# Graph attention on one core: row sums by a transposing VectorE sum and a 32-column product, score runs of four key tiles on three PSUM buffers, fixed issue order

## The chip, the core and the metric

The kernel runs on one core of a Trainium2 chip. The metric is the device time of one execution in microseconds (us). Three runs of the kernel before took 3753.75, 3755.6 and 3756.18 us.

The engines are named as in the profile: PE multiplies matrices (PEld is its weight load), DVE is the vector engine, ACT the scalar engine, POOL the general-purpose engine, SP the engine whose queue issues all DMAs here. Each engine works through its own instructions in order and waits on semaphores for the others. PE writes to PSUM, from which DVE and ACT read; POOL reads and writes SBUF.

## What is computed

A layer norm with ReLU, then attention with eight heads of 64 over a graph's adjacency, and a residual add. `x` is 16 x 1024 x 512, `adj` 1024 x 1024, the weights 512 x 512, all float32.

```python
def reference(x, adj, Wq, bq, Wk, bk, Wv, bv):
    h = jnp.maximum(_layernorm(x), 0.0)
    q, k, v = ((h @ W + b).reshape(16, 1024, 8, 64) for W, b in ((Wq, bq), (Wk, bk), (Wv, bv)))
    scores = jnp.einsum('bihd,bjhd->bhij', q, k) / jnp.sqrt(jnp.float32(64))
    scores = scores + jnp.where(adj == 0, -1e9, 0.0)[None, None, :, :]
    weights = jax.nn.softmax(scores, axis=-1)
    return x + jnp.einsum('bhij,bjhd->bihd', weights, v).reshape(16, 1024, 512)
```

## The kernel before

`main_path` does everything; after it, `all_rows_fine` checks the row sums, and `general_path` stands ready for data whose sums are out of bounds, which these are not.

An iteration `i` (there are 128: 16 images, 4 pairs of heads, 2 halves of the queries) works on one image `b`, one pair of heads `p` and 512 queries `qh`. For each of the eight key tiles `kt`, `scores` (L159 to L173) makes a score tile of 128 keys by 2 heads by 512 queries: PE makes two products of 64 rows each (L164), one for each head, which lie on different halves of PE's rows; DVE adds the mask on the way out of PSUM (L167); ACT takes the exponential in place (L168); POOL adds the tile into an accumulator `a` of 128 by 1024 (L171, L173). The scores lie transposed, keys on the partitions, so the sum over the keys is a sum over tiles and then over partitions.

One iteration later, `weighted_sum` (L175) multiplies the eight tiles by V into one PSUM tile `po` (L182: 32 instructions, two abreast in different column halves) and multiplies the accumulator by a matrix of ones (L193, `pr`), so that every one of 64 rows of the result holds the sum over the partitions. ACT copies both out (L195, L197). `finish` (L205) turns the sums (L209, `prt`) and the output (L218, `pot`) into rows of queries by PE transposes; DVE takes the sums (L212), their reciprocals (L214) and the scaled output (L220), POOL adds the residual `xr` (L225), SP stores it.

Between the scores stand fillers that prepare what comes next: three projections an iteration in most (L133 `pk`, L140 `pq`, L149 `pv`, eight instructions of 512 columns each), the transposes of the next image's normed `x` (L125 `pht`, out by ACT, L126), and its loads and norm (`load_norm`: load, statistics on DVE, power on POOL, shift on DVE, ReLU on ACT). `fillers(i)` deals them over the four quarters of an iteration, each behind two score tiles. This is the order in which the program is written; a scheduler then orders each engine's instructions, and may move one between the two products of a score tile.

PSUM has eight banks: two score tiles of two banks each (`ps_s`), one bank for `po` and one for `pr` (`ps_o`), and two for everything else (`ps_a`, tag `acc`): the projections and all transposes take these two in turn. A tile's owner has to wait until the engine that reads the last one but one has done so.

Of the kernel before, what the change touches and what calls it, by code (L numbers as in the profile page):

```python
# [36 lines left out]
def main_path(tc, x, adj, Wq, bq, Wk, bk, Wv, bv, out, sums):  # L37
# [9 lines left out]
    with ExitStack() as ctx:  # L47
        pool = lambda name, bufs=1, **k: ctx.enter_context(tc.tile_pool(name=name, bufs=bufs, **k))
        const = pool("const")
        xpool = pool("xpool", 4)  # L50
# [12 lines left out]
        X, HT, Q, K, V = {}, {}, {}, {}, {}  # L63
# [10 lines left out]
        ones = const.tile([P, HD], F32, tag="ones", name="ones")  # L74
        nc.gpsimd.memset(ones, 1.0)
# [30 lines left out]
        def norm(b, t):  # L106
# [3 lines left out]
            shift = small.tile([P, 1], F32, tag="shift", name=f"shift_{b}_{t}")  # L110
            nc.vector.bn_stats(st, X[b, t])  # L111
            nc.vector.bn_aggr(mv, st)
            nc.vector.tensor_scalar_add(rstd, mv[:, 1:2], EPS)
            nc.gpsimd.tensor_tensor(rstd, rstd, minus_half, ALU.pow)
            nc.vector.scalar_tensor_tensor(shift, mv[:, 0:1], -1.0, rstd, op0=ALU.mult, op1=ALU.mult)  # L115
            nc.scalar.activation(X[b, t], X[b, t], AF.Relu, bias=shift, scale=rstd)  # L116
# [36 lines left out]
        PR, ACC, OT, RS, XR = {}, {}, {}, {}, {}  # L153
# [21 lines left out]
        def weighted_sum(i):  # L175
            b, p, qh = where(i)
            po = ps_o.tile([P, 512], F32, tag="o", name=f"po_{i}")
# [11 lines left out]
            pr_sum = ps_o.tile([P, 512], F32, tag="r", name=f"pr_{i}")  # L189
            acc = ACC.pop(i)  # L190
            for r in range(2):
                rows = slice(r * HD, r * HD + HD)
                nc.tensor.matmul(pr_sum[rows, :], ones, acc[:, r, :], start=True, stop=True)  # L193
# [10 lines left out]

        def finish(i):  # L205
            pt = ps_a.tile([P, TH, P], F32, tag="acc", name=f"prt_{i}")
            rs = RS.pop(i)
            for t in range(TH):
                nc.tensor.transpose(pt[:, t, :], rs[:, ts(t, P)], ident)  # L209
            s = sums[:, i, :]  # L210

            nc.vector.tensor_scalar(s.rearrange("q (t r) -> q t r", r=2), pt[:, :, 0:P:HD], 2.0**-60, None, op0=ALU.max)  # L212
            inv = small.tile([P, 2 * TH], F32, tag="inv", name=f"inv_{i}")
            nc.vector.reciprocal(inv, s)  # L214
            pt = ps_a.tile([P, TH, P], F32, tag="acc", name=f"pot_{i}")
            ot = OT.pop(i)
            for t in range(TH):
                nc.tensor.transpose(pt[:, t, :], ot[:, ts(t, P)], ident)  # L218
            o = work.tile([P, TH, P], F32, tag="o", name=f"o_{i}")
            nc.vector.tensor_mul(  # L220
                o.rearrange("q t (r d) -> q (t r) d", r=2),
                pt.rearrange("q t (r d) -> q (t r) d", r=2),
                inv[:, :, None].to_broadcast([P, 2 * TH, HD]),
            )
            nc.gpsimd.tensor_tensor(o, o, XR.pop(i), ALU.add)  # L225
            nc.sync.dma_start(rows_of(out, i), o)


        def fillers(i):

# [13 lines left out]
            out = [[], [], [], []]  # L244
            for place, g in zip((0, 2, 3), groups):
                out[place].append(g)
            if i:
                out[1].append((weighted_sum, i - 1))
                out[2].append((finish, i - 1))
            flips = {0: (0, 1), 1: (2,), 2: (3,), 3: (4,), 4: (5,), 5: (6, 7)}  # L250
            if b + 1 < B:
                for n, t in enumerate(flips.get(j, ())):
                    out[0 if n == 0 else 3].insert(0, (flip, b + 1, t))

                for t in ((2, 3), (4,), (5,), (6,), (7,), ())[j] if j < 6 else ():
                    out[1].append((load_norm, b + 1, t))
            if j == 6 and b + 2 < B:
                out[1] += [(load_norm, b + 2, 0)]
            if j == 7 and b + 2 < B:
                out[1] += [(load_norm, b + 2, 1)]  # L260
            return out

        def load_norm(b, t):
            load_x(b, t)
            norm(b, t)


        for t in range(NT):
            if t >= 2:
                load_x(0, t)  # L270
            norm(0, t)
# [10 lines left out]
        if B > 1:  # L282
            load_norm(1, 0)
            load_norm(1, 1)
# [9 lines left out]
        weighted_sum(total - 1)  # L294
        finish(total - 1)

# [180 lines left out]
```

## Time and profile before

| | |
|---|---|
| median of three runs | 3755.6 us |
| the profiled execution's own time | 3754.31 us |
| its span, first to last instruction | 3752.5 us |
| granted PE clock | 0.998 |
| PE busy | 3711.6 us, 99% |
| POOL busy | 2337.1 us, 62% |
| DVE busy | 1657.9 us, 44% |
| ACT busy | 1482.8 us, 40% |
| first weighted sum starts at | 109.8 us |

The profile comes from one execution. A row of a group gives line, engine, operation, output and inputs, shape and count, then the busy time in us, the mean ns of one instruction, and the engine's idle time ahead of them with what ended it. A row of a timeline gives start, length, engine, line, operation and count, and in brackets the idle time before it. PE's lengths include the drain of its pipe, so neighbours overlap; the time that a piece takes of PE is the next piece's start less its own.

### The profile page before, as it was taken

How to read it: one execution, taken by the hardware profiler on the slowest of the kernel's cores; microseconds unless marked ns; L12 is line 12 of the kernel's file. 1: busy time of each engine (PE TensorE's matmuls, PEld its weight loads, DVE VectorE, ACT ScalarE, POOL GpSimd, SP SyncE). 2: the span in 40 equal slices, each digit the busy share in tenths (PEclk: the TensorE clock that was granted, in tenths of full speed). 3: DMA queues.
4: the chain of work that ended last, by engine and by line, in shares of the span. 5: the costliest groups of instructions: out<-in, count | busy, mean ns of one | idle time of the engine just before them, and what ended most of it. 6: DMA issues, size and time to landing. Idle time of an engine off the chain costs nothing.

```text
span 3752.5 us, 34865 instructions
## 1 busy us (share of the span) xinstructions
PE 3711.6 (99%) x13378; PEld 1437.4 (38%) x13378; DVE 1657.9 (44%) x2190; ACT 1482.8 (40%) x1681; POOL 2337.1 (62%) x1161
## 2 busy tenths in 40 slices
PE   7999999999999999999999999999999999999998
PEld 3333333333333333333333333333333333333333
DVE  3444444444444444444444444444444444443444
ACT  3433434343343334334333343343433434333343
POOL 1666666666666666666666666666666666666676
PEclk9999999999999999999999999999999999999999
DMA  3001001000100010001000110010101001100000
GB/s 124 26 28 29 26 27 33 23 29 27 32 26 23 29 34 26 26 23 35 27 26 26 30 30 26 26 31 26 29 26 31 29 23 29 31 29 17 17 23 24
DMA packets 157709, 110.58 MB, mean 29 GB/s; under 512 B 7392, under 2 KB 138464, under 8 KB 157536
## 3 DMA queue, kind: packets, MB, share of 16 engines
q1 hardware_dynamic: 157536, 108.30, 9.8%
q8 instruction: 106, 1.74, 0.2%
q14 instruction: 67, 0.55, 0.0%
HBM read 74.72 MB, written 33.55 MB: 29 GB/s over the span
## 4 chain that ended last, share of the span: by engine, by line
PE 98%; DVE 1%; issue 0%; DMA 0%; POOL 0%; SPq 0%; ACT 0%; DVEq 0%; POOLq 0%; ACTq 0%
PE ps L164 29%; PE po L182 24%; PE pk L133 12%; PE pv L149 12%; PE pq L140 12%; PE pr L193 3%; PE pot L218 2%; PE pht L125 2%; PE prt L209 1%; DVE p L167 0%; DMA x<-in_x_dram 0%; PE pmask L102 0%; POOL a L173 0%; SPq L90 0%; SPq L83 0%
## 5 line engine op out<-in xcount | busy, mean ns | idle before, releaser
L173 POOL TENSOR_TENSOR a<-a,p 128x1024 f32<-128x1024 f32 x768 | 1808.4, 2355 | 1017.7 <-ACT p L168 987.0
L167 DVE TENSOR_TENSOR p<-ps,mask 128x1024 f32<-128x1024 f32 x1024 | 1206.2, 1219 | 1093.6 <-PE ps L164 1093.1
L168 ACT ACTIVATE p<-p 128x1024 f32<-128x1024 f32 x1024 | 1082.3, 1057 | 1210.7 <-DVE p L167 1182.2
L164 PE MATMUL ps<-qT,kT 64*128 64x512 f32 x4096 | 1157.9, 619 | 4.8 <-DVE p L167 4.8
L182 PE MATMUL po<-p,v 128*64 128x512 f32 x4096 | 907.2, 595 | 0.0
L164 PEld LDWEIGHTS ps<-qT,kT 64*128 64x128 f32 x4096 | 386.6, 185 | 590.1 <-issue 504.0
L171 POOL TENSOR_TENSOR a<-p,p 128x1024 f32<-128x1024 f32 x128 | 300.9, 2350 | 353.1 <-ACT p L168 353.1
L182 PEld LDWEIGHTS po<-p,v 128*64 128x64 f32 x4096 | 282.8, 137 | 608.7 <-issue 595.0
L133 PE MATMUL pk<-hT,wk 128*128 128x512 f32 x1024 | 471.9, 604 | 0.2 <-ACT mask L103 0.2
L149 PE MATMUL pv<-wv,hT 128*128 128x512 f32 x1024 | 470.2, 603 | 0.0
L140 PE MATMUL pq<-hT,wq 128*128 128x512 f32 x1024 | 464.4, 596 | 0.0
L133 PEld LDWEIGHTS pk<-hT,wk 128*128 128x128 f32 x1024 | 184.1, 189 | 268.7 <-issue 267.5
L149 PEld LDWEIGHTS pv<-wv,hT 128*128 128x128 f32 x1024 | 184.6, 190 | 266.6 <-issue 266.6
L140 PEld LDWEIGHTS pq<-hT,wq 128*128 128x128 f32 x1024 | 184.5, 190 | 212.2 <-issue 212.2
L116 ACT ACTIVATE x<-x,shift,rstd 128x512 f32<-128x512 f32 x128 | 103.8, 813 | 386.2 <-DVE shift L115 382.8
L195 ACT COPY ot<-po 128x512 f32<-128x512 f32 x128 | 74.9, 585 | 455.3 <-PE po L182 455.3
L150 DVE TENSOR_TENSOR v<-pv,bv_rows 128x512 f32<-128x512 f32 x128 | 88.4, 690 | 242.6 <-PE pv L149 242.6
L111 DVE BATCH_NORM_STATS2 st<-x 128x6 f32<-128x512 f32 x128 | 88.5, 691 | 221.2 <-DMA x<-in_x_dram 221.2
L225 POOL TENSOR_TENSOR o<-o,xr 128x512 f32<-128x512 f32 x128 | 162.4, 1269 | 2.5 <-DVE o L220 0.7
L220 DVE TENSOR_TENSOR o<-pot,inv 128x512 f32<-128x512 f32 x128 | 88.5, 692 | 142.2 <-PE pot L218 141.7
L134 ACT ACTIVATE kT<-pk,bk_cols 128x512 f32<-128x512 f32 x128 | 87.9, 687 | 126.6 <-PE pk L133 126.6
L193 PE MATMUL pr<-a,ones 128*64 128x512 f32 x512 | 131.7, 593 | 2.6 <-POOL a L173 2.6
(38 smaller groups left out, 920.1 us busy)
## 6 DMA issues: line engine op xcount, KB each, us to landing
x<-in_x_dram SPq DMA_DIRECT2D x128, 256.0 KB, 2.6
xr<-in_x_dram SPq DMA_DIRECT2D x128, 256.0 KB, 3.0
out_dram<-o SPq DMA_DIRECT2D x128, 256.0 KB, 2.2
adj<-in_adj_dram SPq DMA_DIRECT2D x8, 512.0 KB, 7.1
wk<-in_L_gnn_Wk_dram SPq DMA_DIRECT2D x1, 1024.0 KB, 7.3
wq<-in_L_gnn_Wq_dram SPq DMA_DIRECT2D x1, 1024.0 KB, 9.3
wv<-in_L_gnn_Wv_dram SPq DMA_DIRECT2D x1, 1024.0 KB, 11.5
bv_rows<-in_L_gnn_bv_dram SPq DMA_DIRECT2D x1, 256.0 KB, 10.0
```

Of the source, the lines that this page charges most:

```text
L116: nc.scalar.activation(X[b, t], X[b, t], AF.Relu, bias=shift, scale=rstd)
L133: nc.tensor.matmul(acc, W["k"][:, c, ts(p, P)], HT[b, hf][:, c, :], start=(c == 0), stop=(c == DC - 1))
L140: nc.tensor.matmul(acc, W["q"][:, c, ts(p, P)], HT[b, hf][:, c, :], start=(c == 0), stop=(c == DC - 1))
L149: nc.tensor.matmul(acc, HT[b, hf][:, c, ts(tt, P)], W["v"][:, c, :], start=(c == 0), stop=(c == DC - 1))
L164: nc.tensor.matmul(ps[:, r, :], K[b, p][rows, ts(kt, P)], Q[b, p, qh][rows, :], start=True, stop=True)
L167: nc.vector.tensor_tensor(pr, ps, m[:, None, :].to_broadcast([P, 2, 512]), ALU.add)
L168: nc.scalar.activation(pr, pr, AF.Exp, scale=HD**-0.5)
L171: nc.gpsimd.tensor_tensor(ACC[i], PR[i, 0], pr, ALU.add)
L173: nc.gpsimd.tensor_tensor(ACC[i], ACC[i], pr, ALU.add)
L182: nc.tensor.matmul(po[rows, :], V[b][:, kt, p * P + r * HD : p * P + r * HD + HD], pr[:, r, :], start=(kt == 0), stop=(kt == NT - 1),)
L193: nc.tensor.matmul(pr_sum[rows, :], ones, acc[:, r, :], start=True, stop=True)
L225: nc.gpsimd.tensor_tensor(o, o, XR.pop(i), ALU.add)
```

## The change

- **Row sums.** `pr` and its 64-column products with ones are gone, as are its copy by ACT and the four PE transposes `prt`. Instead DVE sums the accumulator with `apply_transpose`: each block of 32 by 32 is transposed and summed along what had been the partitions, which leaves 128 x 32 partial sums `rs`, one for each quarter of the partitions. A new step `row_sums` adds the quarters by one product of 32 columns with a 128 x 128 matrix `same` (one where two indices agree modulo 32); DVE picks each query's own quarter out of it (`picked`), sums, and takes the reciprocal.
- **PSUM.** Three score tiles instead of two. `ps_o` is gone; `po` takes its turn in `ps_a`.
- **Order.** An iteration has two halves of four score tiles each. Behind the first come the x transpose, one projection, the weighted sum of the iteration before, its DVE sum, a second x transpose if there is one, the statistics, and loads; behind the second the row sums, the norm, two projections and the output. PE, DVE, ACT and POOL keep this order as written (`manual_schedule`); SP is still scheduled.
- **Loads** of `x` are issued an iteration ahead of their statistics, from five buffers instead of four; the norm is split into `stats` and `norm`.

```diff
-        xpool = pool("xpool", 4)
+        xpool = pool("xpool", 5)
...
-        ps_s = pool("ps_s", 2, space=psum)
-        ps_o = pool("ps_o", 1, space=psum)
+        ps_s = pool("ps_s", 3, space=psum)
...
+        nc.vector.tensor_reduce(place, ident.rearrange("p (g q) -> p q g", q=32), AX.X, ALU.add)
+        nc.vector.tensor_reduce(group, ident.rearrange("p (g q) -> p g q", q=32), AX.X, ALU.add)
+        nc.vector.tensor_copy(same.rearrange("p (g q) -> p g q", q=32), place[:, None, :].to_broadcast([P, 4, 32]))
+        nc.vector.tensor_copy(own, group[:, None, :].to_broadcast([P, 2 * TH, 4]))
...
         def weighted_sum(i):
             b, p, qh = where(i)
-            po = ps_o.tile([P, 512], F32, tag="o", name=f"po_{i}")
+            po = ps_a.tile([P, 512], F32, tag="acc", name=f"po_{i}")
...
-            pr_sum = ps_o.tile([P, 512], F32, tag="r", name=f"pr_{i}")
-            acc = ACC.pop(i)
-            for r in range(2):
-                rows = slice(r * HD, r * HD + HD)
-                nc.tensor.matmul(pr_sum[rows, :], ones, acc[:, r, :], start=True, stop=True)
+            RS[i] = small.tile([P, 4 * 2 * TH], F32, tag="rs", name=f"rs_{i}")
+            acc = ACC.pop(i).rearrange("p r (c q) -> p (r c) q", q=32)
+            nc.vector.tensor_reduce(RS[i], acc, AX.X, ALU.add, apply_transpose=True)
             OT[i] = work.tile([P, 512], F32, tag="ot", name=f"ot_{i}")
             nc.scalar.copy(OT[i], po)
-            RS[i] = work.tile([P, 512], F32, tag="rs", name=f"rs_{i}")
-            nc.scalar.copy(RS[i], pr_sum)
...
+        def row_sums(i):
+            pt = ps_a.tile([P, 2 * TH, 4], F32, tag="acc", name=f"pr_{i}")
+            nc.tensor.matmul(pt.rearrange("q a g -> q (a g)"), same, RS.pop(i), start=True, stop=True)
+            s = sums[:, i, :]
+            picked = small.tile([P, 2 * TH, 4], F32, tag="picked", name=f"picked_{i}")
+            nc.vector.scalar_tensor_tensor(picked, pt, 2.0**-60, own, op0=ALU.max, op1=ALU.mult)
+            nc.vector.tensor_reduce(s, picked, AX.X, ALU.add)
+            INV[i] = small.tile([P, 2 * TH], F32, tag="inv", name=f"inv_{i}")
+            nc.vector.reciprocal(INV[i], s)
...
         def finish(i):
-            pt = ps_a.tile([P, TH, P], F32, tag="acc", name=f"prt_{i}")
-            rs = RS.pop(i)
-            for t in range(TH):
-                nc.tensor.transpose(pt[:, t, :], rs[:, ts(t, P)], ident)
...
+        LOADS = ((4,), (5,), (6,), (7,), (), (0,), (1,), (2, 3))
+        STATS = ((2, 3), (4,), (5,), (6,), (7,), (), (0,), (1,))
+        FLIPS = ((0, 1), (2,), (3,), (4,), (5,), (6, 7), (), ())
...
+            first = flips[:1] + groups[:1]
             if i:
+                first.append((weighted_sum, i - 1))
+            first += flips[1:] + [(stats, *bt) for bt in normed] + loads
+            second = [(row_sums, i - 1)] if i else []
+            second += [(norm, *bt) for bt in normed] + groups[1:]
+            if i:
+                second.append((finish, i - 1))
+            return first, second
...
-        for i in range(total):
-            fill = fillers(i)
-            for quarter in range(4):
-                scores(i, 2 * quarter)
-                scores(i, 2 * quarter + 1)
-                for f, *a in fill[quarter]:
-                    f(*a)
+        with tc.manual_schedule(engines={engines.PE, engines.DVE, engines.Activation, engines.Pool}):
+            for i in range(total):
+                fill = fillers(i)
+                for half in range(2):
+                    for kt in range(half * NT // 2, (half + 1) * NT // 2):
+                        scores(i, kt)
+                    for f, *a in fill[half]:
+                        f(*a)
```

PE before, in the third iteration of the first image, from the product with ones to the second `pk` (a row is one line of the program, `x2` its products; numbers at the ends of names are the program's own):

```order
L193 MATMUL pr_784<-a_601,ones 64x512 x2
L164 MATMUL ps_4_805<-qT_1_0_609,kT_1_556 128x512 x2
L164 MATMUL ps_5_812<-qT_1_0_609,kT_1_556 128x512 x2
L133 MATMUL pk_2_0_820<-hT_0_131,wk 128x512 x4
L209 MATMUL prt_826<-ident,rs_789 128x128 x4
L164 MATMUL ps_6_843<-qT_1_0_609,kT_1_556 128x512
L218 MATMUL pot_834<-ident,ot_787 128x128 x4
L164 MATMUL ps_6_843<-qT_1_0_609,kT_1_556 128x512
L164 MATMUL ps_7_850<-qT_1_0_609,kT_1_556 128x512 x2
L133 MATMUL pk_2_1_857<-hT_1_202,wk 128x512 x4
```

PE now, in the same iteration, from the last rows of the weighted sum to the next iteration's first score tile:

```order
L192 MATMUL po_770<-p_7_693,v_406 64x512 x2
L174 MATMUL ps_4_802<-qT_1_0_630,kT_1_583 128x512 x2
L174 MATMUL ps_5_809<-qT_1_0_630,kT_1_583 128x512 x2
L174 MATMUL ps_6_816<-qT_1_0_630,kT_1_583 128x512 x2
L174 MATMUL ps_7_823<-qT_1_0_630,kT_1_583 128x512 x2
L215 MATMUL pr_830<-rs_787,same 128x32
L143 MATMUL pk_2_0_841<-hT_0_134,wk 128x512 x4
L143 MATMUL pk_2_1_847<-hT_1_205,wk 128x512 x4
L229 MATMUL pot_853<-ident,ot_789 128x128 x4
L174 MATMUL ps_0_862<-qT_1_1_763,kT_1_583 128x512 x2
```

Four score tiles stand together and whole, where there were two, then one cut in two by `pot`, then one; `prt` is gone, and `pr` is one product of 32 columns behind the run.

DVE before, in the same iteration, from the statistics of `x` to the output's scaling (`p` is a mask add, `qT` a projection's way out of PSUM):

```order
L111 BN_STATS st_7_1069<-x_7_1067 128x6
L112 BN_AGGR mv_7_1070<-st_7_1069 128x2
L113 TENSOR_SCALAR rstd_7_1071<-mv_7_1070 128x1
L141 TENSOR_SCALAR qT_1_1_746<-pq_1_1_747,bq_cols 128x512
L115 SCALAR_TENSOR_TENSOR shift_7_1072<-mv_7_1070,rstd_7_1071 128x1
L167 TENSOR_TENSOR p_2_756<-ps_2_753,mask 128x1024
L167 TENSOR_TENSOR p_3_763<-ps_3_760,mask 128x1024
L167 TENSOR_TENSOR p_4_808<-ps_4_805,mask 128x1024
L167 TENSOR_TENSOR p_5_815<-ps_5_812,mask 128x1024
L212 TENSOR_SCALAR sums<-prt_826 128x8
L214 RECIPROCAL inv_832<-sums 128x8
L220 TENSOR_TENSOR o_839<-pot_834,inv_832 128x512
```

DVE now, from the last add of the first half to the work on the row sums:

```order
L177 TENSOR_TENSOR p_3_753<-ps_3_750,mask 128x1024
L151 TENSOR_SCALAR qT_1_1_763<-pq_1_1_764,bq_cols 128x512
L202 TENSOR_REDUCE rs_787<-a_608 128x32
L116 BN_STATS st_5_793<-x_5_667 128x6
L117 BN_AGGR mv_5_794<-st_5_793 128x2
L118 TENSOR_SCALAR rstd_5_795<-mv_5_794 128x1
L177 TENSOR_TENSOR p_4_805<-ps_4_802,mask 128x1024
L177 TENSOR_TENSOR p_5_812<-ps_5_809,mask 128x1024
L177 TENSOR_TENSOR p_6_819<-ps_6_816,mask 128x1024
L177 TENSOR_TENSOR p_7_826<-ps_7_823,mask 128x1024
L219 SCALAR_TENSOR_TENSOR picked_832<-pr_830,own 128x32
L220 TENSOR_REDUCE sums<-picked_832 128x8
```

The new sum of the accumulator stands between the way out of `qT` and the second half's adds, and the work on the sums behind the last add; the shift has moved behind them too.

More of the change, by code (lines that the diff above doesn't have):

```diff
@@ L114, in norm @@
             nc.gpsimd.tensor_tensor(rstd, rstd, minus_half, ALU.pow)
+            MV[b, t], RSTD[b, t] = mv, rstd
+        def norm(b, t):
+            mv, rstd = MV.pop((b, t)), RSTD.pop((b, t))
+            shift = small.tile([P, 1], F32, tag="shift", name=f"shift_{b}_{t}")
             nc.vector.scalar_tensor_tensor(shift, mv[:, 0:1], -1.0, rstd, op0=ALU.mult, op1=ALU.mult)
@@ L220, in finish @@
             nc.vector.tensor_mul(
[L221 to L223 removed]
+                o.rearrange("q t (r d) -> q t r d", r=2),
+                pt.rearrange("q t (r d) -> q t r d", r=2),
+                inv.rearrange("q (r t) -> q t r", r=2)[:, :, :, None].to_broadcast([P, TH, 2, HD]),
             )
```

56 lines of the change are left out of this document (23 added, 33 removed).

## The prediction

> **What bounds the kernel now.** I read the page first: the engines' busy times and the chain of work that ended last.
>
> ```profile
> span 3752.5 us, 34865 instructions
> PE 3711.6 (99%) x13378; PEld 1437.4 (38%) x13378; DVE 1657.9 (44%) x2190; ACT 1482.8 (40%) x1681; POOL 2337.1 (62%) x1161
> PE 98%; DVE 1%; issue 0%; DMA 0%; POOL 0%; SPq 0%; ACT 0%; DVEq 0%; POOLq 0%; ACTq 0%
> PE ps L164 29%; PE po L182 24%; PE pk L133 12%; PE pv L149 12%; PE pq L140 12%; PE pr L193 3%; PE pot L218 2%; PE pht L125 2%; PE prt L209 1%; DVE p L167 0%; DMA x<-in_x_dram 0%; PE pmask L102 0%; POOL a L173 0%; SPq L90 0%; SPq L83 0%
> ```
>
> PE is the chain. Busy can hide waiting, so I asked for the stretch from the first weighted sum to the start of the last, by the windows view:
>
> ```profile
> core 0: us, PE busy (x) PEld busy (x) DVE busy (x) ACT busy (x) POOL busy (x), PEclk, DMA share, GB/s
> 109.83:3729.34 3619.51, 3615.43 (x13059) 1391.85 (x13057) 1612.90 (x2093) 1439.96 (x1622) 2301.39 (x1126) 1.00 0.09 27
> ```
>
> These are 127 iterations of 3619.51/127 = 28.50 us (28.9 in the full ones, below), at full clock, with 4 us of PE idle in all. So only PE's own order and amount of work can pay, and only as long as no other engine makes PE wait. The timeline of PE over one full iteration shows what the 28.90 us go to (start, length, what; pieces overlap by their drain, so I use differences of starts):
>
> ```profile
> 695.70 1.99 PE L164 MATMUL ps<-qT,kT 64*128 64x512 f32 x8
> 697.61 3.70 PE L149 MATMUL pv<-wv,hT 128*128 128x512 f32 x8
> 701.15 0.60 PE L209 MATMUL prt<-ident,rs 128*128 128x128 f32 x4
> 701.68 1.12 PE L164 MATMUL ps<-qT,kT 64*128 64x512 f32 x2
> 702.74 0.66 PE L218 MATMUL pot<-ident,ot 128*128 128x128 f32 x4
> 703.32 1.98 PE L164 MATMUL ps<-qT,kT 64*128 64x512 f32 x6
> 705.23 0.66 PE L125 MATMUL pht<-ident,x 128*128 128x128 f32 x4
> 705.73 3.60 PE L149 MATMUL pv<-wv,hT 128*128 128x512 f32 x8
> 709.25 1.99 PE L164 MATMUL ps<-qT,kT 64*128 64x512 f32 x8
> 711.17 3.70 PE L140 MATMUL pq<-hT,wq 128*128 128x512 f32 x8
> 714.80 1.99 PE L164 MATMUL ps<-qT,kT 64*128 64x512 f32 x8
> 716.72 7.09 PE L182 MATMUL po<-p,v 128*64 128x512 f32 x32
> 723.64 1.03 PE L193 MATMUL pr<-a,ones 128*64 128x512 f32 x4
> 724.60 0.70 PE L164 MATMUL ps<-qT,kT 64*128 64x512 f32 x2
> ```
>
> The beat of a 512-column step is in the weight loads of the weighted sum, which come two abreast (one pair of 64-column products a step):
>
> ```profile
> 688.73 0.14 PEld L182 LDWEIGHTS po<-p,v 128*64 128x64 f32 x2 [0.29 <-issue]
> 689.16 0.14 PEld L182 LDWEIGHTS po<-p,v 128*64 128x64 f32 x2 [0.29 <-issue]
> ```
>
> So a step is 0.43 us. A score tile is four instructions in two steps, its two 64-row products side by side. Three things stand out. A run of two tiles (x8) takes 1.92, four steps (1.72) and 0.20: the price of entering and leaving the 64-row mode, about 0.10 at each end (pr before scores shows one end: 0.96 against two steps, 0.86). The tile that the output transposes (pot) cut in two takes 1.06 for its lone half, two steps and the mode's price; the x6 behind pot takes as long as x8. And pr and prt are PE work for row sums alone.
>
> **The change, part by part.**
>
> PE's scores. Today an iteration has five runs: 1.91 + 1.06 + 1.91 + 1.92 + 1.92 = 8.72. In the new fixed order there are two runs of four whole tiles: 2 x (8 x 0.43 + 0.20) = 7.28. Saved 1.44.
>
> Row sums on PE. pr goes: 0.96, of which 0.10 is the mode's price that the weighted sum now pays on its way to the scores: saved 0.86. prt goes: 0.53 + 0.58 for prt and pot now, against 0.44 + 0.09 for pot alone with one exit: saved 0.58. The projections no longer each border a run: 3.54 + 3.52 + 3.63 = 10.69 against 3.43 + 3.43 + 3.53: saved 0.30. New is the product of 32 columns with the 128x128 weights "same": two instructions. No row shows such a form. The nearest are a transpose of 128 columns, four steps in 0.44 (pht above: 705.23 to 705.73, with 0.06 for the mode), so 0.11 each, and the closing count's product of 2 columns:
>
> ```profile
> L419 PE MATMUL c_n<-c_both,c_ones 128*1 128x2 f32 x2 | 0.2, 164 | 3.3 <-issue 3.3
> ```
>
> Both of its instructions end within 0.2 us. I take two steps of 0.11 and 0.03 for the waiting weights, 0.25, and 0.10 for entering full mode in the projections' place: 0.35; ends 0.1 and 0.6. [...]
>
> Together 1.44 + 0.86 + 0.58 + 0.30 - 0.35 = 2.83 us an iteration. Two iterations in eight have a second x transpose between weighted sum and scores, 0.2 each, 0.05 on the mean.
>
> Does a wait take it back? Durations and latencies that decide this:
>
> ```profile
> L173 POOL TENSOR_TENSOR a<-a,p 128x1024 f32<-128x1024 f32 x768 | 1808.4, 2355 | 1017.7 <-ACT p L168 987.0
> L168 ACT ACTIVATE p<-p 128x1024 f32<-128x1024 f32 x1024 | 1082.3, 1057 | 1210.7 <-DVE p L167 1182.2
> L225 POOL TENSOR_TENSOR o<-o,xr 128x512 f32<-128x512 f32 x128 | 162.4, 1269 | 2.5 <-DVE o L220 0.7
> L114 POOL TENSOR_TENSOR rstd<-rstd,minus_half 128x1 f32<-128x1 f32 x128 | 70.0, 548 | 30.1 <-DVE rstd L113 29.9 <-DVE shift L115 0.2
> L126 ACT COPY hT<-pht 128x512 f32<-128x512 f32 x128 | 72.7, 568 | 30.5 <-PE pht L125 30.5
> L111 DVE BATCH_NORM_STATS2 st<-x 128x6 f32<-128x512 f32 x128 | 88.5, 691 | 221.2 <-DMA x<-in_x_dram 221.2
> L167 DVE TENSOR_TENSOR p<-ps,mask 128x1024 f32<-128x1024 f32 x1024 | 1206.2, 1219 | 1093.6 <-PE ps L164 1093.1
> L411 DVE TENSOR_REDUCE c_both<-sums 128x1 f32<-128x1024 f32 x1 | 1.2, 1209 | 0.0
> L214 DVE RECIPROCAL inv<-sums 128x8 f32<-128x8 f32 x128 | 26.0, 203 | 4.4
> L212 DVE TENSOR_SCALAR sums<-prt 128x8 f32<-128x8 f32 x128 | 20.5, 160 | 164.5 <-PE prt L209 164.5
> ```
>
> And from the DVE timeline, how soon it follows PE (scores from 695.70, pot from 702.74, pq from 711.17), with a place near the end where runs stand close and two buffers run out, and the whole of such waits from the waits view (total, times, longest):
>
> ```profile
> 696.94 2.36 DVE L167 TENSOR_TENSOR p<-ps,mask 128x1024 f32<-128x1024 f32 x2 [6.59 <-PE ps L164]
> 703.43 0.69 DVE L220 TENSOR_TENSOR o<-pot,inv 128x512 f32<-128x512 f32 x1 [1.07 <-PE pot L218]
> 714.91 0.75 DVE L141 TENSOR_SCALAR qT<-pq,bq_cols 128x512 f32<-128x512 f32 x1
> 3589.13 2.34 DVE L167 TENSOR_TENSOR p<-ps,mask 128x1024 f32<-128x1024 f32 x2
> 3590.39 0.30 PEld L164 LDWEIGHTS ps<-qT,kT 64*128 64x128 f32 x4 [1.78 <-DVE p L167]
> 3590.39 2.26 PE L164 MATMUL ps<-qT,kT 64*128 64x512 f32 x8 [0.95 <-DVE p L167]
> PE ps L164 <- DVE p L167: 4.8, 6, 1.0
> ```
>
> *Fourth tile of a run.* Let a run start at 0. The first mask add starts at 1.24 (695.70 to 696.94) and ends at 2.46; two adds in 2.36 mean one each 1.14. PE reaches tile four at 0.10 + 6 x 0.43 = 2.68. Released PE loads weights 0.04 after the add's end (3589.13 + 1.22, then 3590.39), so at 2.50, and needs 0.10 more: 2.60. With three buffers the wait is nothing, by a margin of 0.08 alone. In the first run of an iteration pot's multiply stands ahead on DVE: it starts 0.69 after pot, ends at 1.38, and the run's first add is due at 0.53 + 1.24 = 1.77 on that clock. Covered by 0.4. If the margin fails, a run pays at most 0.27 (2.26 against 1.99 above).
>
> *The weighted sum's PSUM.* It now shares two buffers with the projections and takes the one that the x transpose left, which ACT copies out behind all four exponentials: adds end at 1.24 + 3 x 1.14 + 1.22 = 5.88, the last exponential at 6.97, the copy at 7.55. PE is there at 3.64 + 0.50 + 3.53 = 7.67. Margin 0.12; nothing counted, up to 0.2 in the upper bound. ACT is relieved of the rs copy.
>
> *DVE's sum.* Behind qT on DVE (starts at 4.14 + 3.74 = 7.88, ends 8.6) stand the transposing sum of 1024 columns and the statistics (0.69 and two small ones of the size of the sums' rows, 1.0), before the second run's first add at 7.67 + 7.0 + 1.24 = 15.9. The sum may last 15.9 - 8.6 - 1.0 = 6.3 us before it delays anything. The row of the plain 1024-column reduce says 1.2, which I take; a transposing one is in no row, so the upper end is open (a rival, below). It waits for POOL's last add: POOL needs 7 x 2.35 + 0.55 + 1.27 = 18.3 of 26.1 us, starts the second run's four adds at 14.7 + 3.6 = 18.3 and ends them at 27.8, 1.7 into the next iteration; DVE asks at 8.6. Hidden. The three small operations on the sums come behind the last add of the second run: the first, which frees the PSUM buffer, ends at about 6.1 from that run's start, and the second projection, which takes the buffer, is due at 3.64 + 0.35 + 3.43 = 7.4.
>
> *Loads.* They are issued one iteration ahead of their statistics, with five buffers, and SP has them ahead of the output stores that wait for POOL; DVE's waits for x (221 us in the st row) were hidden and go. Worth nothing; if SP held one back, DVE would stand before the second run's adds with the slack of 6.3 - 1.2 = 5.1 us.
>
> I put the small margins at 0.03 a run. An iteration then saves 2.83 - 0.05 - 0.06 = 2.72. In the last eight intervals there are few projections or none; eight score tiles then follow each other and DVE's 1.14 a tile rules against 0.86, so I count half there: 119 x 2.72 + 8 x 1.36 = 335. Prologue and tail: nothing. The profiled execution took 3754.3 (span 3752.5), so 3754.3 - 335 = 3419; the median of the runs is 1.3 above that execution, which makes **3420 us**, 9% less.
>
> Bounds: all waits nil and the small product at its 0.1 gives 0.25 + 0.06 more, 39 us, 3381; both runs paying 0.27, the weighted sum 0.2 and the product 0.6 takes 0.54 + 0.2 + 0.25 = 1.0 us, 126, up to 3546 if all come together.
>
> **Rivals.**
>
> *New waits inside the runs.* DVE lags by a few tenths in every run (through pot's multiply, v's evacuation or a slower release), and PE stands at the fourth tile or at the weighted sum. For it: margins of 0.08 and 0.12, in-order queues. Against: only six such waits before, 4.8 us. At 0.4 a run, 0.8 an iteration: 3420 + 102 = 3522.
>
> *DVE becomes the bound: slower.* If the transposing sum works its 32 blocks one at a time, its price is 32 times a small instruction. From 6.3 us each further us costs 127; from 6.3 + 2.7 = 9.0 the kernel is slower than now. At 32 x 0.33 = 10.6 us: 3420 + 4.3 x 127 = 3966. For it: no row has the form. Against: the plain reduce is 1.2, and DVE's smallest rows (0.16 to 0.2) would give 6.4 even block by block. [...]
>
> *No change.* The gain is eaten exactly: a sum of about 9 us, or waits of 2.7 an iteration. 3754. That the change might not do what it says is excluded by the two orders, which show whole tiles and no pr or prt.
>
> **How the numbers follow.** Forecast (3380 to 3460) 0.72; waits in the runs (3460 to 3600) 0.20; slower 0.05; no change 0.03. The range 3380 to 3495 takes in the forecast and the nearer half of the first rival, 0.82. Faster by over 0.2% (7.5 us, what a measurement of this kernel can tell from none): 0.92; within: 0.03; slower: 0.05.
>
> **What would show it.** Right: the weighted sums start 26.1 us apart in full iterations; a run x16 of scores takes 3.64; the small product under 0.4; the transposing sum about 1.2; PE's waits for DVE stay under 20 us in all. Wrong: score rows on PE with idle time released by DVE's mask add; a sum above 6 us; PE waiting on POOL for row sums.

## The result, and the profile after

The changed kernel takes 3402.35 us (median of four runs, 3402.22 to 3403.19), the kernel before 3754.68 us beside it: a ratio of 0.906, interval 0.9046 to 0.9078. It is 9.4% faster; the forecast was 3420, 9% less. The profiled execution's span is 3400.4 us against 3752.5, 352.1 less.

From the page of the profile after, its busy times, its chain and four groups (line, engine, operation, shape and count; busy us, mean ns of one; idle us ahead of them and what ended it):

```profile
PE 3359.0 (99%) x12610; PEld 1365.5 (40%) x12610; DVE 1998.0 (59%) x2450; ACT 1414.9 (42%) x1553; POOL 2338.3 (69%) x1160
PE 97%; DVE 1%; POOL 1%; issue 1%; SPq 0%; DMA 0%; ACT 0%; DVEq 0%; POOLq 0%; ACTq 0%
L174 PE MATMUL ps<-qT,kT 64*128 64x512 f32 x4096 | 953.2, 603 | 5.3 <-DVE p L177 5.2
L183 POOL TENSOR_TENSOR a<-a,p 128x1024 f32<-128x1024 f32 x768 | 1811.3, 2359 | 782.8 <-ACT p L178 732.6
L202 DVE TRANSPOSE_TENSOR_REDUCE rs<-a 128x32 f32<-128x1024 f32 x128 | 158.0, 1234 | 9.8 <-POOL a L183 9.8
L125 DVE SCALAR_TENSOR_TENSOR shift<-mv,rstd 128x1 f32<-128x1 f32 x128 | 226.3, 1777 | 2.6 <-POOL rstd L119 2.6
```

PE still is the chain, and its busy time fell by 352.6 us, which is the whole difference of the spans. So nothing was gained from waits and next to nothing lost to them: over all 4096 score instructions PE stood 5.2 us for DVE's mask add. The transposing sum takes 1.234 us. One row is odd: `shift`, an operation on one column, takes 1777 ns where it took 159; it comes up again below.

PE's timeline over one full iteration after (start, length, what), from the small product of one iteration to that of the next:

```profile
640.36 0.41 PE L215 MATMUL pr<-rs,same 128*128 128x32 f32 x2
640.60 7.11 PE L159 MATMUL pv<-wv,hT 128*128 128x512 f32 x16
647.55 0.60 PE L229 MATMUL pot<-ident,ot 128*128 128x128 f32 x4
648.08 3.70 PE L174 MATMUL ps<-qT,kT 64*128 64x512 f32 x16
651.72 3.70 PE L150 MATMUL pq<-hT,wq 128*128 128x512 f32 x8
655.35 7.09 PE L192 MATMUL po<-p,v 128*64 128x512 f32 x32
662.37 3.70 PE L174 MATMUL ps<-qT,kT 64*128 64x512 f32 x16
666.00 0.41 PE L215 MATMUL pr<-rs,same 128*128 128x32 f32 x2
```

Read by differences of starts: a run of four tiles (x16) takes 3.64 and 3.63, the small product 0.24, pot 0.53, and from product to product it is 25.64 us (an iteration without an x transpose). DVE's timeline in the second half of the same stretch:

```profile
655.46 0.75 DVE L151 TENSOR_SCALAR qT<-pq,bq_cols 128x512 f32<-128x512 f32 x1 [1.51 <-PE pq L150]
656.12 1.24 DVE L202 TRANSPOSE_TENSOR_REDUCE rs<-a 128x32 f32<-128x1024 f32 x1
657.28 0.65 DVE L116 BATCH_NORM_STATS2 st<-x 128x6 f32<-128x512 f32 x1
...
663.61 4.62 DVE L177 TENSOR_TENSOR p<-ps,mask 128x1024 f32<-128x1024 f32 x4 [5.27 <-PE ps L174]
668.70 2.24 DVE L125 SCALAR_TENSOR_TENSOR shift<-mv,rstd 128x1 f32<-128x1 f32 x1
```

The sum follows qT without a wait, and behind the statistics DVE stands idle for 5.27 us until the next run's first tile: the slack in which a longer sum would disappear. The windows view splits the stretch between the first and the last weighted sum at the 120th, for the kernel before and for the one after (us, PE busy, clock, DMA share, GB/s):

```profile
109.83:3548.13 3438.30, 3438.30 (x12370) 1.00 0.09 27
3548.13:3729.34 181.21, 177.13 (x691) 1.00 0.07 21
```

```profile
107.36:3211.38 3104.02, 3103.87 (x11656) 1.00 0.10 30
3211.38:3378.08 166.70, 160.81 (x642) 1.00 0.08 23
```

Over 119 intervals the mean goes from 28.89 to 26.08 us: 334.3 us saved. The last eight save 14.5, the prologue 2.5 (the first weighted sum starts at 107.36 instead of 109.83), the tail 0.8.

### The profile page after: what moved, and what is told of

It is laid out like the page before. It is cut to its first block, busy times and chain, and to the rows that moved or that the text cites. A ratio compares the mean times of both kernels' runs of the same rounds, so it can differ in the third digit from the quotient of the medians.

```text
span 3400.4 us, 33496 instructions
## 1 busy us (share of the span) xinstructions
PE 3359.0 (99%) x12610; PEld 1365.5 (40%) x12610; DVE 1998.0 (59%) x2450; ACT 1414.9 (42%) x1553; POOL 2338.3 (69%) x1160
## 4 chain that ended last, share of the span: by engine, by line
PE 97%; DVE 1%; POOL 1%; issue 1%; SPq 0%; DMA 0%; ACT 0%; DVEq 0%; POOLq 0%; ACTq 0%
PE ps L174 27%; PE po L192 26%; PE pq L150 13%; PE pk L143 13%; PE pv L159 13%; PE pht L135 2%; PE pot L229 2%; PE pr L215 1%; POOL a L183 1%; DVE p L177 0%; PE pmask L108 0%; DMA x<-in_x_dram 0%; SPq L89 0%; DVE st L116 0%; SPq L96 0%
## 5 line engine op out<-in xcount | busy, mean ns | idle before, releaser
L177 DVE TENSOR_TENSOR p<-ps,mask 128x1024 f32<-128x1024 f32 x1024 | 1182.2, 1217 | 750.7 <-PE ps L174 750.7
L174 PE MATMUL ps<-qT,kT 64*128 64x512 f32 x4096 | 953.2, 603 | 5.3 <-DVE p L177 5.2
L174 PEld LDWEIGHTS ps<-qT,kT 64*128 64x128 f32 x4096 | 365.1, 186 | 486.7 <-issue 346.2
L143 PE MATMUL pk<-hT,wk 128*128 128x512 f32 x1024 | 455.3, 597 | 0.0
L159 PE MATMUL pv<-wv,hT 128*128 128x512 f32 x1024 | 454.4, 597 | 0.0
L151 DVE TENSOR_SCALAR qT<-pq,bq_cols 128x512 f32<-128x512 f32 x128 | 96.1, 751 | 235.0 <-PE pq L150 235.0
L125 DVE SCALAR_TENSOR_TENSOR shift<-mv,rstd 128x1 f32<-128x1 f32 x128 | 226.3, 1777 | 2.6 <-POOL rstd L119 2.6
L202 DVE TRANSPOSE_TENSOR_REDUCE rs<-a 128x32 f32<-128x1024 f32 x128 | 158.0, 1234 | 9.8 <-POOL a L183 9.8
```

The costliest lines, as they stand in the source:

```text
L143: nc.tensor.matmul(acc, W["k"][:, c, ts(p, P)], HT[b, hf][:, c, :], start=(c == 0), stop=(c == DC - 1))
L159: nc.tensor.matmul(acc, HT[b, hf][:, c, ts(tt, P)], W["v"][:, c, :], start=(c == 0), stop=(c == DC - 1))
L174: nc.tensor.matmul(ps[:, r, :], K[b, p][rows, ts(kt, P)], Q[b, p, qh][rows, :], start=True, stop=True)
L177: nc.vector.tensor_tensor(pr, ps, m[:, None, :].to_broadcast([P, 2, 512]), ALU.add)
L202: nc.vector.tensor_reduce(RS[i], acc, AX.X, ALU.add, apply_transpose=True)
```

## The experiments

Each was timed beside the kernel before, whose medians lay between 3753.3 and 3753.8. The theory: PE's order and amount of work pay, term by term as in the prediction, and the fixed order and the third buffer only keep the other engines out of its way. The rivals: the row sums alone bring most of it; DVE's sum or its place is close to becoming the bound; the order is worth nothing.

| label | kernel | us | ratio to before, interval |
|---|---|---|---|
| row_sums_only | before, with the new row sums | 3696.34 | 0.985 (0.9819 to 0.9876) |
| runs_only | after, with the old row sums | 3528.30 | 0.940 (0.9373 to 0.9427) |
| runs_of_two | after, score runs of two tiles | 3471.53 | 0.925 (0.9222 to 0.9276) |
| runs_of_two_two_buffers | the same on two score buffers | 3474.94 | 0.926 (0.9231 to 0.9284) |
| two_score_buffers | after, on two score buffers | 3672.41 | 0.978 (0.9755 to 0.9812) |
| product_x3 | after, small product three times | 3457.66 | 0.921 (0.9192 to 0.9229) |
| sum_x5 | after, DVE's sum five times | 3407.87 | 0.908 (0.906 to 0.9096) |
| sum_x8 | after, DVE's sum eight times | 4075.26 | 1.086 (1.0834 to 1.0877) |
| shift_one_tensor | after, another form of `shift` | 3400.98 | 0.906 (0.9045 to 0.9075) |
| sum_early | after, DVE's sum half an iteration earlier | 4355.98 | 1.161 (1.1571 to 1.1638) |
| scheduler_free | after, order not fixed | 4072.37 | 1.085 (1.0818 to 1.0881) |

### The row sums alone

The new row sums put into the kernel before, with its scheduler and its PSUM pools. Without `prt` its scheduler leaves the score tiles whole, in four runs of two:

```diff
-            nc.tensor.matmul(pr_sum[rows, :], ones, acc[:, r, :], start=True, stop=True)
...
+            nc.vector.tensor_reduce(RS[i], acc, AX.X, ALU.add, apply_transpose=True)
...
-                out[2].append((finish, i - 1))
+                out[2] += [(row_sums, i - 1), (finish, i - 1)]
```

> The kernel before (two score buffers, quarters, scheduled order) with the new row sums alone: no products with ones, no copy of them, no prt; the transposing sum, the 32-column product and the three small operations instead. Theory A (PE's time is its steps of 0.43 us plus about 0.19 for each score run's mode, and everything else is hidden): pr saves 0.86 an iteration. Without prt the scheduler no longer cuts a score tile in two, so there are four runs of 1.92 instead of 8.72 in five: 1.04. The stretch pv, prt, half tile, pot of 4.65 becomes pv, pr, pot of 4.30: 0.35. Together 2.25 x 127 = 286, 3470 us. Theory B (the gain comes of the longer runs, the third buffer and the fixed order): 3755 less pr alone, some 3640.

Measured 3696.34: 57 us gained, where theory A's count of PE's work gave about 284. Neither theory forecast this; both lay lower (3470 and 3640). Two rows of its waits view (us in total, times, longest), a place in its DVE and PE timelines, and the windows row of the projection there (us, PE busy, clock, DMA share, GB/s):

```profile
DVE rs L197 <- POOL a L179: 499.4, 105, 7.4
PE pq L146 <- DVE v L156: 108.9, 44, 2.5
```

```profile
752.45 1.25 DVE L197 TRANSPOSE_TENSOR_REDUCE rs<-a 128x32 f32<-128x1024 f32 x1 [4.97 <-POOL a L179]
753.62 0.65 DVE L156 TENSOR_TENSOR v<-pv,bv_rows 128x512 f32<-128x512 f32 x1
754.33 5.40 PE L146 MATMUL pq<-hT,wq 128*128 128x512 f32 x8 [2.52 <-DVE v L156]
```

```profile
754.33:759.65 5.32, 5.32 (x8) 0.68 0.01 3
```

The scheduler put the sum on DVE right behind the iteration's last mask add, where POOL's last add is still to come. DVE stands 4.97 us here, 499.4 in all, the evacuation of v waits behind it, and PE waits 2.52 for v's buffer. Then the projection runs at a granted clock of 0.68 and takes 5.40 instead of 3.60. The trace's records of the granted clock hold 35 stretches at 0.5 before its last instructions, 31 of them 3.4 us long and four 6.8. In all PE's idle time is 183.9 us against 40.9 before (108.9 of it for v, 38.4 in 33 waits for the mask add), and PE's busy time fell by 199.6 us where the work removed was forecast at 284, at a granted clock of 0.980 on the mean. So the forecast missed a cost that is not in the sum's 1.25 us, but in where DVE's instructions stand.

### The runs alone

The changed kernel with the old products with ones, their copy by ACT and the four transposes:

```diff
-            nc.vector.tensor_reduce(RS[i], acc, AX.X, ALU.add, apply_transpose=True)
+                nc.tensor.matmul(pr_sum[rows, :], ones, acc[:, r, :], start=True, stop=True)
...
+                nc.tensor.transpose(pt[:, t, :], rs[:, ts(t, P)], ident)
```

> The changed kernel (runs of four, three score buffers, fixed order) with the old row sums: products with ones behind the weighted sum, their copy by ACT, prt at the place of the 32-column product. Theory A: an iteration has the changed kernel's 26.05 us, less 0.24 for the small product, plus 0.86 for pr (in the weighted sum's mode) and 0.44 for prt: 27.1, so 3402 + 1.06 x 127 = 3537 us. Theory B: near the changed kernel's 3402, or with the products' time alone, 3402 + 60.

Measured 3528.30, within 9 us of the forecast. So in the fixed order the new row sums are worth 126 us (3528.3 - 3402.35), 0.99 an iteration; the prediction's terms for them, 0.86 + 0.58 - 0.35 = 1.09, come out within 0.1.

### Runs of two, and the third buffer

The fixed order, but with four runs of two whole tiles, fillers dealt over the four; and then the buffers, in runs of four and of two:

```diff
-                for half in range(2):
-                    for kt in range(half * NT // 2, (half + 1) * NT // 2):
+                for quarter in range(4):
+                    for kt in range(2 * quarter, 2 * quarter + 2):
```

```diff
-        ps_s = pool("ps_s", 3, space=psum)
+        ps_s = pool("ps_s", 2, space=psum)
```

> The changed kernel with its fillers dealt over four places instead of two, so that scores stand in four runs of two whole tiles, in fixed order, with three buffers. The work is the same; an iteration has eight changes of PE's mode instead of five. Theory A: each costs about 0.19 / 2 on either side, so three more are 0.57 us an iteration: 3402 + 72 = 3474 us, the run x8 at 1.92 on the timeline. Theory C (a run's length is free; only the cut tile and the removed products counted): 3402.

> The changed kernel with two score buffers instead of three, the two banks left empty. Theory A: in a run of four, the third tile waits for the first mask add (ends 2.46 after the run's start, PE released at 2.50 instead of 1.82) and the fourth for the second add (released at 3.64 and then starting anew); a run ends at about 4.7 instead of 3.64, which is 2.1 us an iteration, 3402 + 270 = 3670 us. Theory C (DVE keeps up, the third buffer is not needed): 3402.

> Four runs of two whole tiles in fixed order (3472 with three score buffers), with two score buffers. Theory A (a run of two fits two buffers; the third buffer serves only the third and fourth tile of a run): within 10 us of 3472, so the new row sums and whole tiles in a fixed order are worth some 280 us by themselves, as first expected of the row sums alone. Theory F (the third buffer is what hides the mask adds in any run): 100 us or more above 3472.

Measured 3471.53, 3672.41 and 3474.94, all three as forecast by the theory. Runs of two cost 69 us. PE's timeline of runs_of_two shows them as four times 1.91 to 1.92, 7.67 an iteration against 3.64 + 3.63 = 7.27 after:

```profile
648.46 1.99 PE L174 MATMUL ps<-qT,kT 64*128 64x512 f32 x8
650.38 3.70 PE L159 MATMUL pv<-wv,hT 128*128 128x512 f32 x8
654.01 1.99 PE L174 MATMUL ps<-qT,kT 64*128 64x512 f32 x8
655.93 0.41 PE L215 MATMUL pr<-rs,same 128*128 128x32 f32 x2
```

That is 0.40, and where two projections stood in one piece after (6.95), a run now stands between them, which costs another 0.2 (3.63 here, 3.52 for the other). PE stands only 1.1 us for mask adds in the whole kernel: what a run costs is the price of its two ends, 0.20, at the run itself and 0.1 beside it. PE's timeline of two_score_buffers:

```profile
654.14 1.99 PE L174 MATMUL ps<-qT,kT 64*128 64x512 f32 x8
656.66 2.26 PE L174 MATMUL ps<-qT,kT 64*128 64x512 f32 x8 [0.54 <-DVE p L177]
658.85 0.41 PE L215 MATMUL pr<-rs,same 128*128 128x32 f32 x2
```

Without the third buffer a run of four takes 4.71 us (658.85 - 654.14) instead of 3.63, 2.16 an iteration. PE stands before tile three for 0.54, and then each tile has to wait for a mask add. In runs of two the buffer is worth 3.4 us. So the third buffer is not a gain by itself; it is what makes a run of four possible, and without it the longer run is 197 us worse than the shorter one. The last of the three kernels has what row_sums_only has, four runs of two whole tiles, two score buffers and the new row sums, but in the fixed order: it gains 3753.3 - 3474.9 = 278 us, where row_sums_only got 57. What the earlier loads, the fifth buffer for x and the place of `po` have in this was not tried apart.

### The small product three times

```diff
-            nc.tensor.matmul(pt.rearrange("q a g -> q (a g)"), same, RS.pop(i), start=True, stop=True)
+            rs = RS.pop(i)
+            for _ in range(3):
+                nc.tensor.matmul(pt.rearrange("q a g -> q (a g)"), same, rs, start=True, stop=True)
```

> The changed kernel with the 32-column product made three times over. Theory A: two instructions of some 0.11 us each, bound by their weights, so two products more are 0.44 to 0.5 us an iteration, 3402 + 60 = 3462. [...]

Measured 3457.66, so one product more costs (3457.66 - 3402.35) / 2 / 128 = 0.216 us, its two instructions 0.108 each. PE's timeline of product_x3:

```profile
649.54 0.86 PE L217 MATMUL pr<-rs,same 128*128 128x32 f32 x6
650.23 4.97 PE L159 MATMUL pv<-wv,hT 128*128 128x512 f32 x11
```

Six instructions take 0.69 from start to start, two take 0.24. The prediction's step of 0.11, taken from transposes with as many weight columns, was right although only 32 columns stream through. Every instruction of this product has a load of 128 weight columns of its own (256 loads for 256 instructions in the kernel after), and 108 ns is measured. A transpose, in which 128 columns stream, takes as long a step (0.11, four in 0.44), which points to the weight load; it is not shown, since no run keeps the weights in place.

### DVE's sum five and eight times

The same sum, repeated five times in sum_x5 and eight times in sum_x8 (shown), so that DVE's stretch before the second run gets longer and nothing else changes:

```diff
-            nc.vector.tensor_reduce(RS[i], acc, AX.X, ALU.add, apply_transpose=True)
+            for _ in range(8):
+                nc.vector.tensor_reduce(RS[i], acc, AX.X, ALU.add, apply_transpose=True)
```

> The changed kernel with the transposing sum made five times over into the same place, 5 x 1.15 = 5.8 us of DVE an iteration instead of 1.2. Theory A (its cover on DVE is 6.3 us): within 15 us of 3402. Rival (the sum lies on the path that sets the end): each of the four more costs 1.15 x 128, together 590, near 3990.

> The transposing sum made eight times over, 8 x 1.15 = 9.2 us an iteration. Theory A: 2.9 us more than the cover of 6.3, so the second run's first mask add and with it the run's fourth tile come 2.9 late in each iteration: 3402 + 2.9 x 127 = 3770 us, about the kernel before. Rival (no cover worth naming): 3402 + 7 x 1.15 x 128 = 4430. Rival (DVE has 40% idle time, so it is absorbed): 3402.

Five sums, 6.2 us, cost 5.5 us in all: hidden. Eight cost 673, where the forecast of 3770 allowed 368. DVE's and PE's timelines of sum_x8, one tile of the next iteration, and two stretches of its windows (us, the busy time of PE, PEld, DVE, ACT and POOL, clock, DMA share, GB/s), one behind each of the two waits:

```profile
707.25 10.19 DVE L203 TRANSPOSE_TENSOR_REDUCE rs<-a 128x32 f32<-128x1024 f32 x8
718.34 4.62 DVE L177 TENSOR_TENSOR p<-ps,mask 128x1024 f32<-128x1024 f32 x4
719.62 1.13 PE L174 MATMUL ps<-qT,kT 64*128 64x512 f32 x4 [3.29 <-DVE p L177]
721.00 8.73 PE L143 MATMUL pk<-hT,wk 128*128 128x512 f32 x16
749.89 1.13 PE L174 MATMUL ps<-qT,kT 64*128 64x512 f32 x4 [1.69 <-DVE p L177]
```

```profile
721.00:729.57 8.57, 8.57 (x18) 3.72 (x18) 4.54 (x6) 4.29 (x5) 8.33 (x4) 0.81 0.00 0
750.95:759.84 8.89, 8.89 (x20) 3.89 (x19) 3.46 (x7) 3.17 (x3) 8.54 (x4) 0.81 0.00 0
```

The threshold of 6.3 us that the prediction worked out lies between the two (6.2 is all but free, 10.2 is not); the runs don't place it closer. PE fills its three buffers, waits 3.29 us before tile four, and then runs the next two projections at a clock of 0.81 on the mean: 8.57 instead of 6.95. The waits view gives 396.2 us for PE's waits for the mask add, and PE's busy time rose from 3359.0 to 3633.3 for the same work, at a granted clock of 0.935 on the mean instead of 0.998. 396 + 274 = 670 of the 673 us lost. So these waits cost PE 1.7 times themselves.

The wait of 1.69 us is followed by the same clock of 0.81, but not every short wait is. By the clock records, a stretch at 0.5 follows within 6 us behind all 101 waits of 3.3 to 3.7 us before score tiles in this kernel, behind 30 of the 44 waits of 2.5 us in row_sums_only, and behind 9 of the 15 waits of 1.7 us here. In two_score_buffers, whose waits of about 0.5 us stand in every run, none follows them (0.999 on the mean). What sets the clock apart behind waits of one length is not shown.

### The slow `shift`

```diff
-            nc.vector.scalar_tensor_tensor(shift, mv[:, 0:1], -1.0, rstd, op0=ALU.mult, op1=ALU.mult)
+            nc.vector.tensor_scalar(shift, mv[:, 0:1], rstd, -1.0, op0=ALU.mult, op1=ALU.mult)
```

> The changed kernel with the norm's shift, -mean x rstd, written with the mean as the one tensor and rstd as a per-partition scalar, instead of as an operation on two tensors. In the changed kernel's trace the shift takes 1777 ns on the mean, against 159 before. Theory A (with two tensor inputs in SBUF it is held up by a POOL add in flight): the shift falls to about 160 ns and DVE's busy time by 200 us. The time stays within 5 us of 3402, because the shift stands where DVE has slack. Rival (the hold-up is the place in the order, whatever the form): the shift stays near 1777. Rival (the hold-up delays v or the output): some 10 to 30 us faster.

The one group by its line (least, median and most ns; first and last start), in the kernel after and in this one:

```profile
L125 DVE SCALAR_TENSOR_TENSOR shift<-mv,rstd x128: 145/2182/2255, 6.1 to 3121.2; 128x1 f32<-128x1 f32 x128
```

```profile
L125 DVE TENSOR_SCALAR shift<-mv,rstd x128: 160/163/215, 6.0 to 3121.0; 128x1 f32<-128x1 f32 x128
```

The operation is back at 0.16 us, DVE's busy time falls by 201 us, and the kernel takes 3400.98 us, which the measurement can't tell from 3402.35. So the form is the cause, and it lay off the path. In the fixed order `shift` stands behind the second run's mask adds, in the middle of POOL's adds of 2.36 us each. By the trace of the kernel after, 102 of the 128 start 0.12 to 0.20 us into such an add, take 2168 to 2255 ns and end within 0.03 us of the add's end. One starts 2.08 us into an add, takes 305 ns and ends with it, 15 start in the last 0.1 us of one and take 145 to 148, and ten beside none take 152 to 160. Before, none of the 128 lies beside an add, and they take 150 to 161. With one tensor the longest is 215. Why an add holds up this form is not shown.

### The order: one step earlier, and none

First, only DVE's sum is moved, from behind the weighted sum to the second half's list, half an iteration earlier. Second, the fixed order is given up altogether and the scheduler orders the program as the new loops write it:

```diff
-            nc.vector.tensor_reduce(RS[i], acc, AX.X, ALU.add, apply_transpose=True)
...
+        def partial_sums(i):
...
             second = [(row_sums, i - 1)] if i else []
+            second.append((partial_sums, i))
```

```diff
-        with tc.manual_schedule(engines={engines.PE, engines.DVE, engines.Activation, engines.Pool}):
+        if True:
```

> The changed kernel, in its fixed order, with the transposing sum alone moved: it stands on DVE right behind the reciprocal of the same iteration instead of behind the next iteration's first four mask adds. Work and PE's order are the same. Theory D (where the sum stands behind POOL decides; that is what cost the row sums alone their gain under the scheduler): POOL's last add ends about 13.1 after the second run's start, so DVE stands from 6.7 to 13.1 with v, the output and the next run's adds queued behind it. With v on DVE the output transposes start 4.1 late, without it the fourth tile of the next run is 2.3 late, 3.2 on the mean: 3402 + 3.2 x 127 = 3810 us, and up to 3960 if PE's clock falls after such waits as it did with the eightfold sum. Theory E (the sum's place is of no matter, DVE has slack): 3402.

> The changed kernel without the fixed order: the scheduler orders PE, DVE, ACT and POOL. PE's order comes out the same row for row; on DVE the transposing sum stands right behind the reciprocal, ahead of v, the output and the next run's adds. Theory D (the fixed order matters through the sum's place on DVE alone): the same as with the sum moved early, 3810 to 3960 us, slower than the kernel before. Theory E (the fixed order is worth nothing, since PE's order is the same): 3402.

Measured 4355.98 and 4072.37. The direction is as forecast by the theory that the sum's place decides, and the rival by which the order is worth nothing falls; both sizes lie above the range given (3810 to 3960), and the two kernels, forecast alike, differ by 284 us. DVE's, ACT's and PE's timelines of sum_early, in order of time, and a stretch of its windows (us, PE busy, clock, DMA share, GB/s):

```profile
770.58 1.25 DVE L208 TRANSPOSE_TENSOR_REDUCE rs<-a 128x32 f32<-128x1024 f32 x1 [6.95 <-POOL a L183]
771.75 0.12 DVE L125 SCALAR_TENSOR_TENSOR shift<-mv,rstd 128x1 f32<-128x1 f32 x1
771.95 0.81 ACT L126 ACTIVATE x<-x,shift,rstd 128x512 f32<-128x512 f32 x1 [7.78 <-DVE shift L125]
772.67 1.25 ACT L144 ACTIVATE kT<-pk,bk_cols 128x512 f32<-128x512 f32 x2
773.39 1.12 PE L231 MATMUL pot<-ident,ot 128*128 128x128 f32 x4 [5.18 <-ACT kT L144]
774.43 6.13 PE L174 MATMUL ps<-qT,kT 64*128 64x512 f32 x16
```

```profile
773.39:780.50 7.11, 7.11 (x21) 0.58 0.26 74
```

DVE waits 6.95 us for POOL's last add. Behind it in the queues stand `shift`, behind that ACT's norm, behind that the evacuation of kT, and PE's pot needs kT's buffer: 5.18 us of standing, and then transposes and a run of four at a clock of 0.58 (6.07 instead of 3.64 for the run). The waits view puts 312.0 us on kT in 58 waits and 258.8 on v in 60; with 48.8 on the mask adds that is 620, and PE's busy time rose by 341.5 (3700.5 against 3359.0) at a granted clock of 0.907 on the mean: 961 against a loss of 954.

In scheduler_free PE's instructions stand in the same order as after; those of DVE, ACT and POOL differ. Its DVE and PE timelines:

```profile
759.66 2.29 DVE L125 SCALAR_TENSOR_TENSOR shift<-mv,rstd 128x1 f32<-128x1 f32 x1 [1.74 <-POOL rstd L119]
761.87 2.34 DVE L177 TENSOR_TENSOR p<-ps,mask 128x1024 f32<-128x1024 f32 x2
764.36 6.33 PE L159 MATMUL pv<-wv,hT 128*128 128x512 f32 x8 [3.75 <-DVE picked L219]
769.13 1.25 DVE L202 TRANSPOSE_TENSOR_REDUCE rs<-a 128x32 f32<-128x1024 f32 x1 [4.36 <-POOL a L183]
770.30 1.25 DVE L160 TENSOR_TENSOR v<-pv,bv_rows 128x512 f32<-128x512 f32 x2
```

Two faults of this order are to be seen. The sum stands ahead of v again and waits for POOL (814.7 us over the kernel), and PE's output transposes wait for v's buffer (201.5 us). And in two of eight iterations `shift` stands between the mask adds of a run, waits 1.74 for POOL and lasts 2.29, so PE gets its buffer 3.75 us late and works through the next eight instructions in 6.33 instead of 3.6, at a granted clock of 0.60. PE's four largest waits (201.5, 116.7, 52.5, 52.5) are 423, its busy time rose by 254, at a granted clock of 0.935 on the mean: 677 against a loss of 670. What the two would cost one without the other was not tried.

## Why the prediction was right

**What bounds.** PE's order and amount of work, at a granted clock of 0.998 before and after: PE's busy time fell by as much as the span (352.6 and 352.1 us).

**The terms.** A run of four was forecast at 3.64 and takes 3.63 to 3.64; the small product 0.25 without the end that was counted beside it and takes 0.24 (0.216 where it is repeated; no run shows the 0.1 of its lower end); the transposing sum 1.2, measured 1.234. The price of 0.10 at each end of a run explains the 69 us of runs_of_two. pr and prt less the product were 1.09 an iteration, by runs_only 0.99.

**The waits.** The 0.03 a run that was set aside for margins of 0.08 and 0.12 was not needed: PE's waits for the mask add are 5.2 us in all. PE's weight loads do wait there (140.0 us in 263 waits), but the matmuls behind them come in time. The first rival, 0.4 a run, falls; two_score_buffers shows what it would have looked like.

**The second rival.** It did not occur, since the sum takes 1.234 and not 10.6; no row shows the 0.33 a block that the 10.6 comes of. Its threshold of 6.3 agrees with the runs. Its price above that, 127 us for each us, was too low: at 10.2 us the kernel loses 673 us where 127 x 3.9 gives 495, because the clock falls as well, to 0.935 on the mean (PE's waits themselves are 396). On a straight line to that point the kernel would turn slower than before at some 8.3 us, an estimate, and not at the 9.0 it named; no run stands there.

**Where the 17 us are.** The sum came to 335, the span fell by 352.1. In the 119 full intervals 2.81 were saved instead of 2.72: 10.6 us; 0.06 of the 0.09 is what was put down for waits that did not come, and 0.03 the second x transpose, which costs 0.02 and not 0.05. Two other terms were off by more and cancel, which was luck: the projections, by their starts over these intervals, went from 10.70 to 10.51, a saving of 0.19 and not 0.30, and the small product took 0.24 and not 0.35, since the 0.10 for entering the full mode did not show in its time. The last eight intervals gave 14.5 instead of 11, prologue and tail 3.3 instead of nothing. So the whole comes out on the careful side by 17 us. The loads were put at nothing, and DVE's waits for x in front of its statistics did fall from 221.2 to 14.9 us; whether PE gains by it was not tried apart.

**What the prediction did not see.** It weighed the fixed order as the place of each step and put no price on it. It is the part whose loss costs the most: without it the same PE program is 8.5% slower than the kernel before. This holds against the order that this scheduler chose; the kernel before in a fixed order was not tried. And it did not see `shift` slow down, from a median of 159 ns to 2182.

## What to carry to other kernels

When one engine is busy 99%, cost the change in that engine's starts, row by row, and then ask of every queue beside it which instruction will be standing at the head, waiting, and for whom; an instruction of 1.2 us that waits 5 us for a slow engine can hold up what is queued behind it (in row_sums_only the sum's 4.97 us for POOL became 2.52 us of PE's for v). A longer run of one mode paid here only where the buffers let it run through: three buffers and four tiles belong together; four tiles on two buffers lose 197 us to runs of two, and the third buffer under runs of two is worth 3.4. In three of these kernels PE's waits, with the longer work at a lowered clock, cost 1.5 to 1.7 times themselves: 670 us for 396 of waits in sum_x8, 961 for 620 in sum_early, 677 for 423 in scheduler_free. The lowered clock followed some waits of 2.5 and 1.7 us as well (30 of 44 in row_sums_only, 9 of 15 in sum_x8).

## What the runs showed of the hardware that was not expected

- `shift`, an operation on one column with two SBUF tensors, took 2168 to 2255 ns in the 102 of 128 cases in which it started early in a POOL add, and 152 to 160 beside none (after; before, 150 to 161); with one tensor and a per-partition scalar it took 163 on the median (shift_one_tensor).
- The granted clock stood at 0.5 in stretches of 3.4 us (31 of 35 in row_sums_only) or 6.8 (four), behind all 101 PE waits of 3.3 to 3.7 us before score tiles in sum_x8 and some of 1.7 to 2.5 us. In sum_early, behind a wait of 5.18, it was 0.58 on the mean of 7.11 us, and a run of four took 6.07 instead of 3.64.
- The transposing sum of 128 x 1024 fp32 took 1234 ns (after), 2% above the plain reduce's 1209 (before).
- The product of 32 columns with 128 fp32 weight columns is two instructions of 0.108 us each (product_x3), as much as an instruction of a transpose of 128 columns took before (0.11).
